# Linear attention gated by a Hadamard feed-forward, all products by Strassen-Winograd: one more feed-forward unit at two levels, and work moved between VectorE and GpSimd

## The chip, the cores and the metric

The kernel runs on one core of a Trainium2 chip. The metric is the device time of one launch in microseconds. The kernel before took 1565.73 us, the median of three runs (1564.98 to 1567.9). In the text, PE is TensorE, DVE is VectorE, ACT is ScalarE, POOL is GpSimd, SP is the engine whose queue issues the transfers. Everything is float32.

## The reference

Eight sequences of 512 tokens with 512 features. Cut to what is computed:

```python
xn = layernorm(x)                                  # (8, 512, 512)
q, k, v = xn @ Wq.T + bq, xn @ Wk.T + bk, xn @ Wv.T + bv
phi_q, phi_k = elu(q) + 1, elu(k) + 1
context = phi_q * cumsum(phi_k * v, axis=tokens) * 32**-0.5
s = context @ Wo.T + bo
h = fwht(xn * SU_ug)                               # Hadamard transform of 512
up, gate = h @ W_up.T * scale_up, h @ W_gate.T * scale_gate       # 2048 wide
d = fwht(silu(gate) * up * SU_dp) @ W_down.T * scale_dp
out = x + s * silu(d)
```

## The kernel before

**Tiling.** The sequences go in four pairs, p = 0 to 3. In a pair one sequence is one half of the tokens of a matrix product and the other sequence the other half, and each product is done with Winograd's form of Strassen's scheme: seven products P1 to P7 instead of eight. `xo` holds the seven combinations of the tokens, a weight tile `w` the seven combinations of a weight; both are made by `encode_tokens` and `encode_weights` (lines 293 to 308, four additions or subtractions each). The Hadamard transforms are folded into the weights, so only the plain scales remain.

**Groups.** `group` (L442) runs one such scheme: 14 matmuls of 128x512, whose results lie in the PSUM banks px (three buffers), py (one) and pz (two), and are put together by ACT copies (`sa_`, `sb_`, `sc_`, L464) and DVE sums (L468). A matmul appears as two records in the profile. `hidden_unit` (L803) with `block_product` (L622) applies the scheme twice: 7 x 7 x 2 = 98 matmuls of 128x256 do what four `group`s (gate and up, two blocks each) do with 56 of 128x512. It reads weights that were encoded at both levels from DRAM: `w_gu` from `d_gu`, seven pieces of 896 KB for each unit.

**A pair.** `attention` runs k, v, q for two groups of heads: a `group`, then `elu_plus_one` on k and q (relu and exp on ACT, L702 and L703, `add, max` on DVE, L704), v times k (POOL, L716), the cumulative sum as a scan on DVE (L722), and its product with q into `co` (DVE L730), which POOL encodes. Then come four units u of the feed-forward, with the output projection after the first; after unit 1 the first half of the down projection, `down(p, 0)`, and after unit 3 the second, `down(p, 1)` (`token_groups`, L528, L539, L543). The first half's sums `dn`, and the projection `s`, go to DRAM (`d_d`, `d_s`) and come back at the end (L750) as `d` and `s`; `y` is the input again. The last steps are silu(d) on ACT, times s on POOL, plus y on DVE, and the store.

**Pair 0 makes the weights.** There a raw weight is loaded (`raw_w`), k, q, v and o weights are encoded on POOL (`first_w`) and kept in DRAM. `folded_w` loads gate and up weights, makes butterflies on DVE (L930 to L933), multiplies with the Hadamard matrix `had` on PE (L939, bank t), copies with the signs on ACT (L945), and encodes. From two such weights `inner_w` makes the second level (DVE L408) in a tile `s_` of the pool `xin` and stores 14 pieces to `d_gu`. So in pair 0 all four units run with `gate` and `up`, that is with `group`s; `up` multiplies gate and up and POOL encodes the result `ho` (L297 to L300). In pairs 1 to 3 all units are `hidden_unit`s. The down weights are folded in the background by `chain_down`, `butterflies_down` (L969), `fold_down` and `down_w`.

**The next pair's tokens.** `normalized(b)` loads a sequence x_b into the pool `xin`, normalizes it and stores it to `d_x`; `next_tokens` reads it back turned (`squares`, L235: four pieces of 256 KB for each sequence, in runs of 128 bytes) as z_b. The even sequence's z lies in `xin`, the odd one's in `t8`; DVE finishes the transposition (L93) into `xo` while the second down half runs.

**What sets the order.** A place is the time of one matmul of 128x512; `at(n, fn)` writes an agenda of steps that are issued n places later, `advance` runs it. `later` puts DVE work on a list that `pace` issues behind DVE's sums, so much for each; `background` gives a lower priority to the scheduler. Weights come in the order of `queue`; `get_w` asks three ahead. Every transfer is issued by SP in order, so one that waits for a buffer holds those behind it. The pools `wpool` (4 tiles), `t8` (6), `xin` (1), `hop` (2) and `snap` (6) set when a buffer comes free.

Of the kernel before, what the change touches and what calls it, by code (L numbers as in the profile page):

```python
# [21 lines left out]
def kernel(  # L22
# [160 lines left out]
    def normalized(b):  # L183

        xt = load_x(b)
        d = dram.tile([L, D], F32, tag=f"d_x_{b}", name=f"d_x_{b}")
        kept[f"x_{b}"] = d

        def store():
            nc.sync.dma_start(d.rearrange("(n p) d -> p n d", p=P), xt)  # L190

        if b > 3:
            layernorm(b, xt)
            store()
            return
        mv = small.tile([P, NT, 2], F32, tag="mv", name=f"mv_{b}")
        rstd = small.tile([P, NT], F32, tag="rstd", name=f"rstd_{b}")

        def stats(t):
            st = small.tile([P, 6], F32, tag="st", name=f"st_{b}_{t}")  # L200
            nc.vector.bn_stats(st, xt[:, t, :])
            nc.vector.bn_aggr(mv[:, t, :], st)

        def root():
            nc.vector.tensor_scalar(rstd, mv[:, :, 1], EPS, None, ALU.add)
            nc.scalar.activation(rstd, rstd, AF.Sqrt)

        def scaled(t):
            if t == 0:
                nc.vector.reciprocal(rstd, rstd)  # L210
            nc.vector.tensor_scalar(
                xt[:, t, :], xt[:, t, :], mv[:, t, 0:1], rstd[:, t : t + 1], ALU.subtract, ALU.mult
            )

        def start():
            for t in range(NT):
                later(0.8, stats, t)
            later(0.3, root)
            for t in range(NT):
                later(0.6, scaled, t)  # L220
            later(0.0, store)

        at(12, start)
# [115 lines left out]
                w = by_factor(w)  # L339
        return w  # L340

    def raw_w(name, src, n0, dn, step, c0, dc):

        w = new_w(name)
        for a in range(2):
            tiles = src[:, c0 + a * dc : c0 + a * dc + P].rearrange("(n p) e -> p n e", p=P)
            for b in range(2):
                n = n0 + b * dn
                place = (P1, P2, P7, P4)[2 * a + b]
                nc.sync.dma_start(w[:, :, place, :], tiles[:, n : n + step + 1 : step])  # L350
        return w
# [41 lines left out]
    def inner_w(m, u, w0, w1):  # L393

        if u not in inner:
            inner[u] = dram.tile([P, 7, 2, 7, P], F32, tag=f"d_gu_{u}", name=f"d_gu_{u}")
        d = inner[u][:, :, ("gate", "up").index(m)]

        def store(c, t):
            nc.sync.dma_start(d[:, :, c, :], t)  # L400

        store(P1, w0[:, 0])
        store(P2, w0[:, 1])
        store(P4, w1[:, 1])
        t = xin.tile([P, 3, 7, P], F32, tag="x", name=f"s_{m}_{u}")

        def made(c, i, a, b, op):
            nc.vector.tensor_tensor(t[:, i], a, b, op)  # L408
            store(c, t[:, i])

        later(1.0, made, P5, 0, w1[:, 0], w1[:, 1], ALU.add, soon=True)
        later(1.0, made, P6, 1, t[:, 0], w0[:, 0], ALU.subtract, soon=True)
        later(1.0, made, P3, 2, w0[:, 1], t[:, 1], ALU.subtract, soon=True)
        later(1.0, made, P7, 0, w0[:, 0], w1[:, 0], ALU.subtract, soon=True)

# [266 lines left out]
    def attention(p, xo, co, get_w):  # L684
        def project(m, g, then):
            w = get_w(m, g)
            r = t8.tile([P, 2, 2, L], F32, tag="t", name=f"{m}_{p}_{g}")
            b = (col("b" + m, g), col("b" + m, g + 2))

            def whole(px):  # L690
                nc.scalar.activation(r[:, 0, 1], px, AF.Identity, bias=b[0])  # L691
                then(r)

            group(
                f"{m}_{p}_{g}", [w[:, 0], w[:, 1]], x_rhs(xo),
                (r[:, 0, 0], r[:, 1, 0], r[:, 1, 1]), whole, b,
            )

        def elu_plus_one(r, name):
            neg = t8.tile([P, 2, 2, L], F32, tag="t", name=f"neg_{name}")  # L700
            for h in range(2):
                nc.scalar.activation(neg[:, h], r[:, h], AF.Relu, scale=-1.0)  # L702
                nc.scalar.activation(neg[:, h], neg[:, h], AF.Exp, scale=-1.0)  # L703
                nc.vector.scalar_tensor_tensor(r[:, h], r[:, h], 1.0, neg[:, h], ALU.add, ALU.max)  # L704

        def heads(g):
            phi = {}

            def with_k(k):
                phi["k"] = k  # L710
                elu_plus_one(k, f"k_{p}_{g}")

            def with_v(v):
                k = phi["k"]
                for h in range(2):
                    nc.gpsimd.tensor_tensor(v[:, h], v[:, h], k[:, h], ALU.mult)  # L716
                at(4, lambda: sums(k, v))

            def sums(k, v):
                for h in range(2):  # L720
                    for s in range(2):
                        nc.vector.tensor_tensor_scan(  # L722
                            k[:, h, s], ones.to_broadcast([P, L]), v[:, h, s], 0.0, ALU.mult, ALU.add
                        )

            def with_q(q):
                k = phi["k"]
                elu_plus_one(q, f"q_{p}_{g}")
                for h in range(2):
                    nc.vector.scalar_tensor_tensor(  # L730
                        co[:, g, h : h + 3 : 2, :], k[:, h], QSCALE, q[:, h], ALU.mult, ALU.mult
                    )
                encode_tokens(nc.gpsimd, co[:, g])

            project("k", g, with_k)
            project("v", g, with_v)
            project("q", g, with_q)

        for g in range(2):
            heads(g)  # L740
# [43 lines left out]
        )  # L784
        return g

    def up(p, f, g, xo, ho, get_w):

        w = get_w("up", f)
        r = t8.tile([P, 2, 2, L], F32, tag="t", name=f"u_{p}_{f}")  # L790

        def with_up(px):
            nc.gpsimd.tensor_tensor(ho[:, P1], g[:, 0, 0], r[:, 0, 0], ALU.mult)  # L793
            nc.vector.tensor_tensor(ho[:, P7], g[:, 0, 1], px, ALU.mult)
            nc.gpsimd.tensor_tensor(ho[:, P2 : P3 + 1 : 2], g[:, 1], r[:, 1], ALU.mult)
            encode_tokens(nc.gpsimd, ho)

        group(
            f"up_{p}_{f}", [w[:, 0], w[:, 1]], x_rhs(xo),
            (r[:, 0, 0], r[:, 1, 0], r[:, 1, 1]), with_up,  # L800
        )
# [114 lines left out]
        eng.tensor_tensor(d[:, :, 0], s[:, :, 0], s[:, :, 1], ALU.add)  # L916
        eng.tensor_tensor(d[:, :, 1], s[:, :, 0], s[:, :, 1], ALU.subtract)

    def folded_w(name, src, f):

        w = raw_w(f"{name}_{f}", src, 0, 2, 1, f * P, NG * P)
        places = (slice(P1, P7 + 1, 2), slice(P2, P4 + 1, 3))
        rs = []

# [101 lines left out]
    def first_w(m, g):  # L1026


        if m == "gate":
            return folded_w(m, wgate_t, g)  # L1030
        if m == "up":
            return folded_w(m, wup_t, g)
        name, eng = f"{m}_{g}", nc.gpsimd
        if m == "o":
            t = new_w(name)
            w = by_factor(t)
            rows_w(w, wo_t, g, 2)
        else:
            t = w = raw_w(name, sources[m], 0, 2, 1, g * P, 2 * P)

        def encode():
            encode_weights(eng, w)
            keep_w(name, t)

        return w, [(5, encode)]

    def later_w(m, g):
        return stream_w((m, g)), []

# [2 lines left out]
    for p in range(B // 2):  # L1052
        queue += [(p, m, g) for g in range(2) for m in ("k", "v", "q")]
        for u in range(NU):
            if p == 0:
                queue += [(p, m, f) for m in ("gate", "up") for f in (u, u + NU)]
            else:
                queue += [(p, "gu", (u, i)) for i in (P1, P5, P6, P2, P7, P3, P4)]
# [7 lines left out]
    def ask(n):  # L1066
        while queue and len(ahead) < n:
            p, m, g = queue.pop(0)
            w, steps = (first_w if p == 0 and m != "down" else later_w)(m, g)
            ahead.append({"key": (m, g), "w": w, "steps": steps, "traced": 0, "asked": 0, "place": 0})  # L1070

    def step_of(e):
# [88 lines left out]
    for p in range(B // 2):  # L1161
# [9 lines left out]
        more = p + 1 < B // 2  # L1171
        hos = []
        for u in range(NU):
            if p == 0:
                gs = [gate(p, u, xo, get_w)]
                gs.append(gate(p, u + NU, xo, get_w))
                if u == 0:
                    project_out(p, co, get_w)
                ho = hop.tile([P, 2, 7, L], F32, tag="h", name=f"ho_{p}_{u}")
                for m in range(2):  # L1180
                    up(p, u + m * NU, gs[m], xo, ho[:, m], get_w)
            else:
                ho = hop.tile([P, 2, 7, L], F32, tag="h", name=f"ho_{p}_{u}")
                hidden_unit(p, u, xo, ho, get_w, u % 2 == 1)
                if u == 0:
                    project_out(p, co, get_w)
            hos.append(ho)
            if more and u < 2:
                with background():
                    normalized(2 * p + 2 + u)  # L1190
            if u == 1:
                down(p, 0, hos, get_w)
                hos = []
        if more:
            catch_up()
# [57 lines left out]
```

## Time and profile before

| | |
|---|---|
| median of three runs | 1565.73 us |
| the profiled execution's own time | 1565.26 us |
| its span | 1563.5 us |
| mean granted TensorE clock | 0.997 |
| share of the span: PE, PEld, DVE, POOL, ACT | 98%, 71%, 61%, 32%, 27% |
| HBM read, written | 189.83 MB, 76.02 MB |

Stretches of the first pair (busy us of each engine):

| stretch, us | what | PE | DVE | ACT | POOL |
|---|---|---|---|---|---|
| 0 to 50 | load, layernorm, first groups | 41.8 | 30.7 | 22.2 | 23.8 |
| 50 to 100 | attention of pair 0 | 46.6 | 48.9 | 23.3 | 23.0 |
| 100 to 150 | end of attention, unit 0 | 42.0 | 42.2 | 21.9 | 19.2 |
| 150 to 264 | units 0 and 1, first down half begins | 114.0 | 81.4 | 35.7 | 38.1 |
| 264 to 355 | down half, unit 2 | 89.7 | 47.3 | 26.6 | 8.1 |
| 355 to 412 | unit 3 | 53.8 | 43.5 | 16.2 | 23.8 |
| 412 to 470 | second down half | 55.8 | 30.0 | 8.6 | 21.1 |
| 470 to 600 | attention of pair 1 and on | 128.1 | 83.3 | 47.6 | 49.6 |

A row of the timeline gives start, length, engine, line, operation, output tile and input tiles, the form, the number of instructions taken together, and in brackets the idle time before them with what ended it. A row of consecutive matmuls is as long as they take, with a modelled end that reaches a little into the next row; what they take in a stream is read from start to start. Idle time counts here only where it lies on TensorE.

### The profile page before, as it was taken

The page shows a single profiled execution, that of the slowest core. Times are in us where ns is not written, and L with a number is a line of the kernel's source. Part 1 is how long each engine was busy: PE and PEld are TensorE (multiplying, and loading weights), DVE is VectorE, ACT ScalarE, POOL GpSimd, SP SyncE. Part 2 cuts the span into 40 slices and gives each one's busy share as a digit, 9 for nine tenths or more (in the row PEclk, how much of TensorE's full clock was granted, in tenths as well). Part 3 has the DMA queues.
Part 4 walks back from the last instruction along what each step waited for, and adds up shares of the span by engine and source line. Part 5 has one row for each costly group of instructions (what it writes and reads, how often), then busy time and mean ns, then how long its engine had stood idle before and what let it go on. Part 6 is the DMA issues. An engine that isn't in the chain of part 4 may idle for free.

```text
span 1563.5 us, 15520 instructions
## 1 busy us (share of the span) xinstructions
PE 1529.6 (98%) x5840; PEld 1105.7 (71%) x5840; DVE 953.9 (61%) x1336; ACT 419.8 (27%) x666; POOL 501.5 (32%) x286
## 2 busy tenths in 40 slices
PE   7989999999999999999999999999999999999998
PEld 4335546744584588888885488888886468888887
DVE  5898784469466674716676574725675476543673
ACT  5453340232114521112215431111212431111211
POOL 4532144014421252304612235301622226110731
PEclk9999999999999999999999999999999999999999
DMA  8244966566885344344575434335474233535462
GB/s 280 83 148 152 285 227 205 185 199 214 229 305 173 89 161 152 110 159 158 157 283 216 101 138 144 139 101 195 151 250 172 82 106 118 185 98 178 152 251 95
DMA packets 196682, 266.86 MB, mean 171 GB/s; under 512 B 56704, under 2 KB 155008, under 8 KB 192384
## 3 DMA queue, kind: packets, MB, share of 16 engines
q1 hardware_dynamic: 196464, 265.84, 51.8%
q8 instruction: 46, 0.75, 0.2%
q14 instruction: 28, 0.23, 0.0%
q10 hardware_dynamic: 144, 0.03, 0.0%
HBM read 189.83 MB, written 76.02 MB: 170 GB/s over the span
## 4 chain that ended last, share of the span: by engine, by line
PE 88%; DVE 4%; DMA 2%; POOL 2%; ACT 2%; issue 2%; SPq 0%; POOLq 0%; DVEq 0%; ACTq 0%
PE px_gu L630 19%; PE px_dn L528 13%; PE pz_gu L630 9%; PE pz_dn L528 6%; PE py_gu L630 5%; PE py_dn L528 4%; PE px_o L528 3%; PE px_up L452 3%; PE px_k L452 3%; PE px_v L452 3%; PE px_gate L452 3%; PE px_q L452 3%; PE pz_o L528 2%; PE pz_q L452 2%; PE pz_k L452 2%
## 5 line engine op out<-in xcount | busy, mean ns | idle before, releaser
L630 PE MATMUL px_gu<-xo,w_gu 128*128 128x256 f32 x1344 | 320.6, 380 | 0.0
L630 PEld LDWEIGHTS px_gu<-xo,w_gu 128*128 128x128 f32 x1344 | 254.7, 190 | 39.9 <-issue 3.6
L528 PE MATMUL px_dn<-w_down,ho 128*128 128x256 f32 x1024 | 228.5, 379 | 0.0
L528 PEld LDWEIGHTS px_dn<-w_down,ho 128*128 128x128 f32 x1024 | 194.5, 190 | 28.2 <-issue 2.1
L630 PE MATMUL pz_gu<-xo,w_gu 128*128 128x256 f32 x672 | 172.9, 380 | 0.0
L831 POOL TENSOR_TENSOR u<-u,v 128x1024 f32<-128x1024 f32 x24 | 56.1, 2359 | 354.2 <-DVE u L668 347.5
L630 PEld LDWEIGHTS pz_gu<-xo,w_gu 128*128 128x128 f32 x672 | 127.2, 190 | 18.4 <-DVE a L672 0.9
L528 PE MATMUL pz_dn<-w_down,ho 128*128 128x256 f32 x496 | 112.7, 380 | 2.7 <-POOL ho L300 2.7
L528 PEld LDWEIGHTS pz_dn<-w_down,ho 128*128 128x128 f32 x496 | 93.6, 190 | 17.9 <-POOL ho L300 3.5
L876 POOL TENSOR_TENSOR s<-s,d 128x512 f32<-128x512 f32 x30 | 40.4, 1346 | 152.8 <-ACT d L875 113.7
L716 POOL TENSOR_TENSOR v<-v,k 128x1024 f32<-128x1024 f32 x16 | 43.0, 2686 | 140.4 <-ACT v L691 112.7
L630 PE MATMUL py_gu<-xo,w_gu 128*128 128x256 f32 x336 | 86.2, 379 | 0.0
L630 PEld LDWEIGHTS py_gu<-xo,w_gu 128*128 128x128 f32 x336 | 63.9, 190 | 8.7
L793 POOL TENSOR_TENSOR ho<-g,u 128x512 f32<-128x512 f32 x8 | 12.5, 1557 | 164.6 <-DVE u L468 154.7
L835 POOL TENSOR_TENSOR v<-v,r 128x1024 f32<-128x1024 f32 x24 | 56.2, 2365 | 25.6 <-DVE r L668 25.6
L452 PE MATMUL px_v<-xo,w_v 128*128 128x512 f32 x128 | 60.8, 594 | 1.5 <-ACT sc_v L464 1.5
L875 ACT ACTIVATE d<-d 128x512 f32<-128x512 f32 x31 | 19.5, 630 | 158.3 <-DVE d L543 116.1
L452 PE MATMUL px_k<-xo,w_k 128*128 128x512 f32 x128 | 60.9, 597 | 1.1 <-ACT sa_k L464 1.0
L452 PE MATMUL px_gate<-xo,w_gate 128*128 128x512 f32 x128 | 59.7, 594 | 0.9 <-ACT sc_gate L462 0.9
L452 PE MATMUL px_q<-xo,w_q 128*128 128x512 f32 x128 | 60.1, 592 | 0.0
L452 PE MATMUL px_up<-xo,w_up 128*128 128x512 f32 x128 | 59.3, 592 | 0.0
L528 PE MATMUL px_o<-w_o,co 128*128 128x256 f32 x256 | 58.4, 379 | 0.0
(263 smaller groups left out, 2464.1 us busy)
## 6 DMA issues: line engine op xcount, KB each, us to landing
w_gu<-d_gu SPq DMA_DIRECT2D x84, 896.0 KB, 4.5
w_down<-d_down SPq DMA_DIRECT2D x56, 512.0 KB, 3.5
d_s<-o SPq DMA_DIRECT2D x8, 1024.0 KB, 4.4
d_d<-dn SPq DMA_DIRECT2D x8, 1024.0 KB, 7.6
d<-d_d SPq DMA_DIRECT2D x8, 1024.0 KB, 6.7
s<-d_s SPq DMA_DIRECT2D x8, 1024.0 KB, 7.9
y<-in_x_dram SPq DMA_DIRECT2D x8, 1024.0 KB, 7.8
out_dram<-y SPq DMA_DIRECT2D x15, 512.0 KB, 3.3
```

What stands on the lines that cost most here:

```text
L452: nc.tensor.matmul(p.rearrange("p a t -> p (a t)") if len(r.shape) == 2 else p, ws[k][:, i, :], r, start=(first and k == 0), stop=(k == n ...
L528: nc.tensor.matmul(p[:, c], t[:, (2 * g + c) * P : (2 * g + c + 1) * P], ws[i](k), start=(first and k == 0 and c == cs[0]), stop=(k == n - ...
L630: nc.tensor.matmul(p[:, lane], w[:, lane, i, :], x[:, i, :], start=(first and lane == 0), stop=True, skip_group_check=True,)
L716: nc.gpsimd.tensor_tensor(v[:, h], v[:, h], k[:, h], ALU.mult)
L793: nc.gpsimd.tensor_tensor(ho[:, P1], g[:, 0, 0], r[:, 0, 0], ALU.mult)
L831: nc.gpsimd.tensor_tensor(r[:, m], ru1[:, m], rv[:, m], ALU.add)
L835: nc.gpsimd.tensor_tensor(rv[:, m], rv[:, m], rr[:, m], ALU.add)
L875: nc.scalar.activation(d, d, AF.Silu)
L876: (nc.vector if final and (a, s) == (1, 0) else nc.gpsimd).tensor_tensor(r, r, d, ALU.mult)
```

## The change

1. **Unit 3 of pair 0** becomes a `hidden_unit`. Its four raw weights are loaded into tiles of `t8` and folded during the first down half of pair 0 by a new function, `weights_ahead(NU - 1)`, which is called ahead of `down(p, 0)`; the queue asks for the seven `gu` pieces instead. The second level of `xo` is made after that down half (`inner_tokens`, three subtractions of 128x1792) and ahead of unit 3 (`inner_t3`, seven).
2. **`normalized(3)`** moves from after unit 1 to the beginning of unit 3, in the background, and takes the plain `layernorm` branch.
3. **k times v** is issued on DVE, each half followed by its two scans, without the four places between; it was on POOL.
4. **The second half of the exponential** of k and q (relu, exp, `add, max`, for q also the product into `co`) comes seven places later.
5. **Encoding** the k, q and v weights in pair 0 moves from POOL to DVE; so does encoding `ho` for the second block of unit 1.
6. `inner_w`'s last piece (P7) comes eight places later.

```diff
-        if b > 3:
+        if b > 2:
             layernorm(b, xt)
             store()
             return
...
-        later(1.0, made, P7, 0, w0[:, 0], w1[:, 0], ALU.subtract, soon=True)
+
+        def last():
+            later(1.0, made, P7, 0, w0[:, 0], w1[:, 0], ALU.subtract, soon=True)
+
+        later(0.0, at, 8, last, soon=True)
...
-        def elu_plus_one(r, name):
+        def elu_plus_one(r, name, then=None):
             neg = t8.tile([P, 2, 2, L], F32, tag="t", name=f"neg_{name}")
-            for h in range(2):
+
+            def half(h):
                 nc.scalar.activation(neg[:, h], r[:, h], AF.Relu, scale=-1.0)
                 nc.scalar.activation(neg[:, h], neg[:, h], AF.Exp, scale=-1.0)
                 nc.vector.scalar_tensor_tensor(r[:, h], r[:, h], 1.0, neg[:, h], ALU.add, ALU.max)
+                if then:
+                    then(h)
+
+            half(0)
+            at(7, lambda: half(1))
...
             def with_v(v):
                 k = phi["k"]
                 for h in range(2):
-                    nc.gpsimd.tensor_tensor(v[:, h], v[:, h], k[:, h], ALU.mult)
-                at(4, lambda: sums(k, v))
-
-            def sums(k, v):
-                for h in range(2):
+                    nc.vector.tensor_tensor(v[:, h], v[:, h], k[:, h], ALU.mult)
                     for s in range(2):
                         nc.vector.tensor_tensor_scan(
...
             def with_q(q):
                 k = phi["k"]
-                elu_plus_one(q, f"q_{p}_{g}")
-                for h in range(2):
+
+                def context(h):
                     nc.vector.scalar_tensor_tensor(
                         co[:, g, h : h + 3 : 2, :], k[:, h], QSCALE, q[:, h], ALU.mult, ALU.mult
                     )
-                encode_tokens(nc.gpsimd, co[:, g])
+                    if h == 1:
+                        encode_tokens(nc.gpsimd, co[:, g])
+
+                elu_plus_one(q, f"q_{p}_{g}", context)
...
-            encode_tokens(nc.gpsimd, ho)
+            encode_tokens(nc.vector if last else nc.gpsimd, ho)
...
-    def folded_w(name, src, f):
-
-        w = raw_w(f"{name}_{f}", src, 0, 2, 1, f * P, NG * P)
+    def folded_w(name, src, f, room=None):
+
+        w = raw_w(f"{name}_{f}", src, 0, 2, 1, f * P, NG * P, room)
...
-        name, eng = f"{m}_{g}", nc.gpsimd
+        name, eng = f"{m}_{g}", nc.gpsimd if m == "o" else nc.vector
...
+    def weights_ahead(u):
+
+        def begin(m, src, f):
+            t = t8.tile([P, 2, 7, P], F32, tag="t", name=f"w_{m}_{f}")
+            _, steps = folded_w(m, src, f, t)
+            place = 10
+            for _, step in steps:
+                at(place, step)
+                place += 7
+
+        at_ = 2
+        for m, src in (("gate", wgate_t), ("up", wup_t)):
+            for f in (u, u + NU):
+                at(at_, lambda m=m, src=src, f=f: begin(m, src, f))
+                at_ += 12
...
-            if p == 0:
+            if p == 0 and u < NU - 1:
                 queue += [(p, m, f) for m in ("gate", "up") for f in (u, u + NU)]
...
-            w, steps = (first_w if p == 0 and m != "down" else later_w)(m, g)
+            w, steps = (first_w if p == 0 and m not in ("down", "gu") else later_w)(m, g)
...
-            if p == 0:
+            if p == 0 and u < NU - 1:
                 gs = [gate(p, u, xo, get_w)]
                 gs.append(gate(p, u + NU, xo, get_w))
...
-                    up(p, u + m * NU, gs[m], xo, ho[:, m], get_w)
+                    up(p, u + m * NU, gs[m], xo, ho[:, m], get_w, u % 2 == 1 and m == 1)
             else:
+                if p == 0:
+                    catch_up()
+                    inner_t3(xo, (P1, P5, P6, P2, P7))
+                    at(9, lambda: inner_t3(xo, (P3, P4)))
+                    with background():
+                        normalized(3)
                 ho = hop.tile([P, 2, 7, L], F32, tag="h", name=f"ho_{p}_{u}")
                 hidden_unit(p, u, xo, ho, get_w, u % 2 == 1)
...
-            if more and u < 2:
+            if more and u < 2 and (p, u) != (0, 1):
                 with background():
                     normalized(2 * p + 2 + u)
             if u == 1:
+                if p == 0:
+                    weights_ahead(NU - 1)
                 down(p, 0, hos, get_w)
+                if p == 0:
+                    inner_tokens(xo)
                 hos = []
```

More of the change, by code (lines that the diff above doesn't have):

```diff
@@ L340, in stream_w, with raw_w @@
         return w
-    def raw_w(name, src, n0, dn, step, c0, dc):
-        w = new_w(name)
+    def raw_w(name, src, n0, dn, step, c0, dc, w=None):
+        w = new_w(name) if w is None else w
         for a in range(2):
@@ L785, in gate, with up @@
         return g
-    def up(p, f, g, xo, ho, get_w):
+    def up(p, f, g, xo, ho, get_w, last):
         w = get_w("up", f)
```

## The prediction

> **What bounds the kernel now.** I read the page first, then TensorE's timeline for its gaps, then the stretches of the start, and last the DMA issues around the end of the first pair. Page:
>
> ```profile
> span 1563.5 us, 15520 instructions
> PE 1529.6 (98%) x5840; PEld 1105.7 (71%) x5840; DVE 953.9 (61%) x1336; ACT 419.8 (27%) x666; POOL 501.5 (32%) x286
> ...
> PE   7989999999999999999999999999999999999998
> ```
>
> TensorE is the bound: 1529.6 of 1563.5 us. Time can go only by fewer matmuls or by closing its gaps. These are all of 0.8 us or more between 20 and 1500 us (start, us, what, [idle before <- releaser]), each row from TensorE's timeline:
>
> ```profile
> 58.19 3.62 PE L452 MATMUL pz_q<-xo,w_q 128*128 128x512 f32 x4 [3.40 <-DVE q L468]
> 61.64 1.88 PE L452 MATMUL pz_k<-xo,w_k 128*128 128x512 f32 x4
> ```
> ```profile
> 107.92 2.46 PE L988 MATMUL pwd<-rd,had 128*128 128x512 f32 x4 [3.16 <-ACT w_gate L945]
> ```
> ```profile
> 144.67 1.99 PE L528 MATMUL pz_o<-w_o,co 128*128 128x256 f32 x8 [2.92 <-DVE g L468]
> ```
> ```profile
> 265.47 1.99 PE L528 MATMUL pz_dn<-w_down,ho 128*128 128x256 f32 x8 [1.33 <-POOL ho L300]
> ```
> ```profile
> 363.54 1.95 PE L939 MATMUL pw_gate<-r_gate,had 128*128 128x512 f32 x4 [3.18 <-DVE r_gate L933]
> 365.33 1.88 PE L452 MATMUL px_gate<-xo,w_gate 128*128 128x512 f32 x4
> ```
> ```profile
> 428.90 2.00 PE L528 MATMUL pz_dn<-w_down,ho 128*128 128x256 f32 x8 [1.35 <-POOL ho L300]
> 431.07 3.29 PE L528 MATMUL py_dn<-w_down,ho 128*128 128x256 f32 x14 [0.18 <-DMA w_down<-d_down]
> ```
> ```profile
> 492.78 1.98 PE L452 MATMUL px_v<-xo,w_v 128*128 128x512 f32 x4 [1.51 <-ACT sc_v L464]
> ```
>
> Three smaller ones (1.04 at 116, 0.89 at 134.6, 1.04 at 470) bring them to 20 us. Behind the gaps of 3.40 and 3.16 the matmuls run at half clock for about 3.4 us (58.19 to 61.64 for 4 records that take 1.72 elsewhere: +1.73; after 107.92: +1.80, by the same reading), while the gap of 3.18 at 363 is followed by 4 records in the usual 1.8. From 493 to 1500 us there is no gap, so pairs 1 to 3 can only lose. The start is VectorE's: 48.9 of 50 us busy.
>
> ```profile
> 50.00:100.00 50.00, 46.60 (x106) 20.22 (x105) 48.89 (x48) 23.29 (x42) 22.98 (x11) 0.97 0.30 95
> ```
>
> **Part 1: unit 3 of pair 0 with the scheme applied twice.** It issues four `group`s of 14 matmuls of 128x512 now, two records each: 112 x 0.43 us (1.72 for 4) = 48.1. A `hidden_unit` issues 98 of 128x256: 196 x 0.216 (1.72 for 8) = 42.3. That is -5.8 on the bound. The four fold pairs (1.72 each) move, with their loads, encodes and stores, into the first down half: same work, moved. In unit 3 the fold gap (3.18) and in the second down half the encode gap (1.35) and 0.18 lose their cause: -4.7. The narrower matmul costs nothing by width in these rows: 8 of 256 take what 4 of 512 take.
>
> New at the unit's start: VectorE issues about 14 us of work between units 2 and 3 (encodes, down-weight factors, 7 x 0.72 of `inner_t3`) against 14.6 us of matmuls queued there, and the unit's 7 loads of 896 KB land in 4.5 each, as in pairs 1 to 3, where no unit has a gap: +1 (0 to 3). The piece P7 that is stored 8 places later goes where its reader is a whole down half away: 0.
>
> **Part 2: the end of pair 0, where I expect a new wait.** `normalized(3)` moves into unit 3. Its x and the z of sequence 2 share the single buffer of `xin`, and SP's order becomes: x_3's store, a w_down, eight z loads, the two d fetches, w_down, s, y. Now z starts before the down half:
>
> ```profile
> 403.94 0.71 SPq L235 DMA_DIRECT2D z<-d_x  x1
> 405.09 2.59 SPq L400 DMA_DIRECT2D d_gu<-s_up  x2
> 407.73 12.83 SPq L235 DMA_DIRECT2D z<-d_x  x7
> 420.60 1.98 SPq L750 DMA_DIRECT2D d<-d_d  x2
> 422.68 1.44 SPq L335 DMA_DIRECT2D w_down<-d_down  x2
> ```
> ```profile
> 427.45 0.69 DVE L539 TENSOR_TENSOR sa_dn<-px_dn,d 128x512 f32<-128x512 f32 x1 [1.87 <-DMA d<-d_d]
> ```
>
> The half's first matmul is at 411.68, 7.7 us after the first z; d lands 15.8 after it and VectorE already waits 1.87 for it. In the changed order the w_down in front of z waits for that first matmul, so z can't start before it (offset 0 to 3, by x_3's store landing). Eight z at 1.83 (12.83 for 7) are 14.6; d lands about 7 after its issue (median 7.2 in 395 to 440): 22 to 25 after the half's first matmul. VectorE's transposes, then the sum that frees bank py, stand behind d's first reader: 4 us more, 26 to 29. TensorE needs that bank about 20 in: by pair 1's own end, which has no gap, the second block's py_dn comes at 804.01 against 780.70, 23.3 in; counting the changed order's matmuls gives 19.8. The stall, 26 to 29 less 20 to 23, is 3 to 9; I take 7, since w_down, issued 2 behind d and 8.35 to land, is late by about the same; bounds 2 and 14 (w_down's own lateness, 5, on top of 9). If a gap this long is followed by half clock as those of 3.40 and 3.16 were, and that of 3.18 wasn't, it costs 1.7 more; that is in the upper bound. The page TensorE: Matmul & The Clock Gate, of the Trainium skill, has the rule (Why this matters for your kernels) that an idle gap of over about 3 us brings the half clock back; by it the sum below would be -9.0 instead of -10.7.
>
> **Part 3: first attention (20 to 150 us).** VectorE gains 4 k*v (1.17 each beside an idle GpSimd by L816's 2.35 for two at 786.03; the GpSimd op means 2.69) and 8 of the 24 weight encodes at about 0.42: +8 in 50 to 100. It loses the contention with GpSimd that slows its two-input ops:
>
> ```profile
> 49.78 4.50 DVE L969 TENSOR_TENSOR rd<-rd 128x1024 f32<-128x1024 f32 x2
> 54.21 3.34 DVE L722 TENSOR_TENSOR_SCAN k<-ones,v 128x512 f32<-128x512 f32 x2
> ```
>
> 4.50 against 2.35 for the same shape in pair 1: about 11 us between 40 and 106 by such rows, of which 3 to 4 belong to co's and o's encodes, which stay. So VectorE nets about 0 and stays full. What changes is order: q's first difference now stands where it is ready near 52, before its bank is wanted at 54 (gap 3.40 and 1.73 gone), and w_gate's copies stand ahead of the silu that held them (3.16 and 1.80 gone), 10.1 in all. New waits, by walking the new order with these durations: ScalarE's sc_v behind k's later half (1.2), q of the second head behind scans and k*v (about 2.5), pz_o behind the s_gate store (about 1). I take 10.1 less 4.7: -5.4. Bounds: -14.9 (the three other gaps here gone too) and +5 (the last two waits 5 each, with clock).
>
> **Part 4: the rest.** 265: encodes on VectorE and two fold pairs in between, -1.3; there VectorE may stand before a raw weight's slot that GpSimd frees: 0 to +3. Start of pair 1: k's later half stands behind sc_v, -1.5 (0 if VectorE's wait for x keeps it). Attentions of pairs 1 to 3: VectorE takes 4.7 us more each but sat idle 3.39 and 2.46 before the scans there waiting for GpSimd, so 0; bounds 0 (no gap to close but the 1.5 counted) and +10 (six heads, each with a gap of 1.7, near the 1.51 at 492.78).
>
> **Sum**: -5.8 -4.7 +1 +7 -5.4 -1.3 -1.5 = -10.7 on the profiled execution, whose time is 1565.26 (span 1563.5 and 1.8 around it), 0.5 under the median 1565.73. That is 1554.6, in the median's frame 1555.
>
> **Rivals.** (a) *All closes*: the stall is at its bound of 2 and the start's gaps go. With the start at -14.9, 1565.7 - 5.8 - 4.7 - 14.9 - 2.8 + 2 = 1539.5; with it at -5.4 and the +1, 1550; half way, 1545. For it: pair 1 ends with the same loads and no gap. Against: it has four of its eight z loaded earlier, and pair 0's d is late already. (b) *The start gives it all back*: part 3 is +1 instead of -5.4: 1561.4. For it: 48.9 of 50. (c) *Slower, by SP's queue at the end of pair 0*: everything there waits in order behind x_3's store, which waits for four background scales on VectorE. Without its stall the sum is -17.7. The 7 stands for a z that starts 1.5 after the half's first matmul, and each us more delays z, d and w_down by one: at 12 the change gains nothing, at 16 it is 1565.7 - 17.7 + 21.5 = 1569.5. For it: scales at background priority have no due time. Against: VectorE was busy 43.5 of 57 us in 355 to 412, with the encodes that leave this stretch. (d) *Attentions of pairs 1 to 3* get the +10: 1565. For it: two VectorE ops more in a chain that evictions wait behind; against: 83.3 of 130 us busy in 470 to 600. (e) That the unit isn't changed at all is excluded: its 98 matmuls stand in the new order.
>
> **How the numbers follow.** Forecast 0.50 (1555, own range 1551 to 1560), (a) 0.15, (b) 0.13, (c) 0.12, (d) 0.10. 0.2% is 3.1 us, about what a measurement here can tell from no change: faster means under 1562.6, slower over 1568.9. Faster: 0.48 + 0.15 + 0.09 + 0.02 = 0.74; slower: 0.10 of (c), 0.03 of (d) and 0.02 of (b): 0.15; same 0.11. The range leaves out half of (a) and most of (c)'s upper part: 1544 to 1568.
>
> **What would show it.** Right: unit 3 as px_gu/pz_gu of 42.3 us, no gap at pw_gate, no q L468 gap near 55, z's first issue at the down half's first matmul, a gap of 5 to 9 at the half's py_dn with d or w_down behind it. Wrong: no such gap (then nearer 1548), or new gaps in 90 to 150 of over 10 in sum, or a gap after 500.

## The result and the profile after

The changed kernel takes 1572.08 us (median of 8 runs, 1569.28 to 1574.43) beside 1567.22 for the kernel before on the same chips: ratio 1.003, 95% interval 1.0018 to 1.0042, that is 3 to 7 us slower. The forecast was 1555 and the range ended at 1568. The two profiled executions lie further apart than the medians, 1571.8 against 1563.5 us of span (granted clock 0.993 against 0.997); the accounting below is of their 8.3 us. Line numbers from here on are those of each kernel's own file: L472 of the changed kernel is L468 of before, L532 is L528, L547 is L543, L634 is L630, L942 is L933.

TensorE's gaps in the changed kernel (TensorE's timeline, rows as before):

```profile
81.81 1.98 PE L456 MATMUL px_v<-xo,w_v 128*128 128x512 f32 x4 [1.76 <-ACT sc_v L468]
104.14 3.39 PE L456 MATMUL px_gate<-xo,w_gate 128*128 128x512 f32 x4 [4.90 <-DVE w_gate L306]
140.78 1.73 PE L948 MATMUL pw_up<-r_up,had 128*128 128x512 f32 x2 [2.31 <-DVE r_up L942]
216.58 1.95 PE L948 MATMUL pw_up<-r_up,had 128*128 128x512 f32 x4 [1.31 <-DVE r_up L942]
261.14 2.86 PE L532 MATMUL pz_dn<-w_down,ho 128*128 128x256 f32 x12 [0.93 <-DVE u L472]
309.73 1.96 PE L948 MATMUL pw_gate<-r_gate,had 128*128 128x512 f32 x4 [2.17 <-DVE r_gate L942]
375.55 1.13 PE L634 MATMUL pz_gu<-xo,w_gu 128*128 128x256 f32 x4 [3.98 <-DVE u L472]
```

and the end of pair 0 with the start of pair 1:

```profile
438.77 1.22 PE L532 MATMUL py_dn<-w_down,ho 128*128 128x256 f32 x2 [6.03 <-DVE d L547]
439.78 6.18 PE L532 MATMUL px_dn<-w_down,ho 128*128 128x256 f32 x16
```
```profile
478.49 3.23 PE L456 MATMUL px_k<-xo,w_k 128*128 128x512 f32 x4 [1.90 <-ACT sa_k L468]
```

The old gaps at 58, 108, 145, 364, 429 and 493 are gone, and those at 265 and 470 are now 0.93 and 1.90. Seven new ones of 1.3 to 6 us stand elsewhere, and several are followed by half clock: the 16 records after 439.78 take 6.02 us to the next row (445.80) instead of 3.45. Nearly all of it is over by 500 us: pair 1's first `hidden_unit` starts at 545.53 against 537.52, 8.0 late, and the span ends 8.3 late.

The chain at the end of pair 0, VectorE's read of d:

```profile
434.46 0.69 DVE L543 TENSOR_TENSOR sa_dn<-px_dn,d 128x512 f32<-128x512 f32 x1 [8.94 <-DMA d<-d_d]
```

and SP's queue (issues and the time they took to issue):

```profile
410.55 0.37 SPq L190 DMA_DIRECT2D d_x<-x  x1
412.33 0.32 SPq L335 DMA_DIRECT2D w_down<-d_down  x1
415.05 6.33 SPq L235 DMA_DIRECT2D z<-d_x  x5
```

x_3's store is issued at 410.55, the first z at 415.05, 2.9 us after the half's first matmul (412.14), and d is there 22.3 after it. Before, the first z was 7.7 ahead of that matmul.

### The profile page after: what moved, and what is told of

Same layout as the page of the kernel before. It is cut to its first block, busy times and chain, and to the rows that moved or that the text cites. A ratio compares the mean times of both kernels' runs of the same rounds, so it can differ in the third digit from the quotient of the medians.

```text
span 1571.8 us, 15701 instructions
## 1 busy us (share of the span) xinstructions
PE 1530.6 (97%) x5924; PEld 1126.4 (72%) x5924; DVE 1003.0 (64%) x1423; ACT 419.2 (27%) x664; POOL 424.0 (27%) x236
## 4 chain that ended last, share of the span: by engine, by line
PE 82%; DVE 10%; DMA 3%; issue 2%; ACT 1%; SPq 1%; POOL 1%; POOLq 0%; DVEq 0%; ACTq 0%
PE px_gu L634 19%; PE px_dn L532 11%; PE pz_gu L634 9%; PE pz_dn L532 5%; PE py_gu L634 5%; PE px_o L532 4%; PE px_k L456 3%; PE py_dn L532 3%; PE px_v L456 3%; PE px_q L456 3%; PE px_gate L456 2%; PE pz_o L532 2%; PE px_up L456 2%; PE pz_k L456 1%; PE pz_q L456 1%
## 5 line engine op out<-in xcount | busy, mean ns | idle before, releaser
L634 PE MATMUL px_gu<-xo,w_gu 128*128 128x256 f32 x1456 | 348.4, 381 | 0.1
L634 PEld LDWEIGHTS px_gu<-xo,w_gu 128*128 128x128 f32 x1456 | 276.9, 191 | 44.5 <-issue 5.0
L532 PE MATMUL px_dn<-w_down,ho 128*128 128x256 f32 x1024 | 231.2, 382 | 0.0
L532 PEld LDWEIGHTS px_dn<-w_down,ho 128*128 128x128 f32 x1024 | 196.4, 192 | 29.5 <-issue 2.4
L634 PE MATMUL pz_gu<-xo,w_gu 128*128 128x256 f32 x728 | 187.6, 380 | 5.3 <-DVE u L472 4.0
L634 PEld LDWEIGHTS pz_gu<-xo,w_gu 128*128 128x128 f32 x728 | 138.1, 190 | 26.4 <-DVE u L472 4.4
L532 PE MATMUL pz_dn<-w_down,ho 128*128 128x256 f32 x496 | 112.4, 379 | 0.9 <-DVE u L472 0.9
L532 PEld LDWEIGHTS pz_dn<-w_down,ho 128*128 128x128 f32 x496 | 93.7, 190 | 15.4 <-DVE u L472 1.3
L634 PE MATMUL py_gu<-xo,w_gu 128*128 128x256 f32 x364 | 93.4, 379 | 0.0
L297 POOL TENSOR_TENSOR co<-co 128x512 f32<-128x512 f32 x8 | 10.2, 1272 | 265.8 <-DVE co L736 265.8
L634 PEld LDWEIGHTS py_gu<-xo,w_gu 128*128 128x128 f32 x364 | 69.2, 190 | 9.4
L532 PE MATMUL py_dn<-w_down,ho 128*128 128x256 f32 x256 | 58.7, 382 | 6.0 <-DVE d L547 6.0
L830 ACT ACTIVATE a<-a,cols_sb 128x512 f32<-128x512 f32 x26 | 18.8, 722 | 156.5 <-DVE a L672 154.7
L532 PE MATMUL px_o<-w_o,co 128*128 128x256 f32 x256 | 58.4, 379 | 0.0
L532 PEld LDWEIGHTS py_dn<-w_down,ho 128*128 128x128 f32 x256 | 48.8, 191 | 13.0 <-DVE d L547 6.4
```

Source lines behind the costliest of these rows:

```text
L297: eng.tensor_tensor(o[..., P5, :], o[..., P7, :], o[..., P1, :], ALU.subtract)
L532: nc.tensor.matmul(p[:, c], t[:, (2 * g + c) * P : (2 * g + c + 1) * P], ws[i](k), start=(first and k == 0 and c == cs[0]), stop=(k == n - ...
L634: nc.tensor.matmul(p[:, lane], w[:, lane, i, :], x[:, i, :], start=(first and lane == 0), stop=True, skip_group_check=True,)
L830: nc.scalar.activation(g[:, m], g[:, m], AF.Silu, scale=col("w_gate", u + m * NU + a * NG))
```

## The experiments

Ratios are to runs of the kernel before on the same chip, with 95% intervals.

**The two halves of the change alone.** `attention_alone` is the kernel before with these lines of the change (cut):

```diff
-            for h in range(2):
+            half(0)
+            at(7, lambda: half(1))
...
-                    nc.gpsimd.tensor_tensor(v[:, h], v[:, h], k[:, h], ALU.mult)
+                    nc.vector.tensor_tensor(v[:, h], v[:, h], k[:, h], ALU.mult)
...
-        name, eng = f"{m}_{g}", nc.gpsimd
+        name, eng = f"{m}_{g}", nc.gpsimd if m == "o" else nc.vector
```

`unit3_alone` is the changed kernel without them.

> The kernel before with the attention parts alone: k*v on VectorE, the second half of the exponential seven places later, the weight encodes of k, q and v on VectorE; unit 3 of pair 0, x_3 and inner_w as before. Theory (read from the gaps of the two profiles): this half of the change gains 2 us by 184 us (landmark 186.34 to 184.09), loses about 1 at the start of pair 1, where sa_k came late after the stall in front of it and not by these parts, so here 0, and nothing in pairs 1 to 3: 2 to 3 us faster than before. Rival (the rest of the loss, the fold waits of 1.3 to 2.2 us behind VectorE at 216 and 309, also comes from VectorE's added work): 0 to 2 us slower. As predicted before the result: 5.4 and 1.5 faster, 6.9.

> The changed kernel with the attention parts undone (k*v and the weight encodes back on GpSimd, both halves of the exponential at once); unit 3 with the scheme twice, x_3 in unit 3, the folds in the first down half stay. Theory: the loss is all here. 1.1 + 3.98 + 0.36 + 0.5 with 1.5 of half clock at the start of unit 3, 6.03 with 3.15 of half clock in the second down half, 3.4 in the folds of the first, against 5.8 + 3.2 + 1.4 + 0.2 gained: 6 to 10 us slower than before, gaps at pz_gu and py_dn as in the changed kernel. Rival (the attention parts fill VectorE and so make the gaps): those gaps shrink, and it is faster than before by up to 10.

`attention_alone`: 0.9968 (0.9956 to 0.998), about 5 us faster, more than expected. The gaps of 3.40, 3.16 and 1.51 are gone; it has new ones of 1.74 at 82 and 4.81 at 104, and 2.31 at 141 is what is left of the 2.92 at 145. `unit3_alone`: 1.005 (1.0036 to 1.0063), about 8 us slower. It has the gaps at pz_gu and py_dn, the latter even longer, from TensorE's timeline:

```profile
377.97 1.16 PE L634 MATMUL pz_gu<-xo,w_gu 128*128 128x256 f32 x4 [3.98 <-DVE u L472]
```
```profile
443.17 1.22 PE L532 MATMUL py_dn<-w_down,ho 128*128 128x256 f32 x2 [8.00 <-DVE d L547]
```

So the loss lies in the half that has less work for TensorE, and the attention's moves were not its cause.

**The chain from x_3's store.** `x3_urgent` takes one thing from the changed kernel:

```diff
-                    with background():
-                        normalized(3)
+                    normalized(3)
```

> The changed kernel with one line less: normalized(3) in unit 3 without the background priority, so that VectorE's four scales and x_3's store come earlier and the z loads of the second down half start ahead of w_down. Theory (the wait is a chain from x_3's store through SP's queue to z, d and bank py): z starts 10 us or more earlier, VectorE's wait of 8.94 for d and TensorE's gap of 6.03 go to under 2, and the half clock behind it (3.15) too: 7 to 10 us faster than the changed kernel, 2 to 5 faster than before. Rival 1 (the transfers themselves are the limit: eight z in runs of 128 bytes, d, s, y, w_down in one stretch): z starts earlier and the gap stays over 4, now behind w_down; 0 to 3 faster. Rival 2: VectorE waits for x_3's load ahead of the sums of unit 3, a new gap of 2 or more there.

0.9943 (0.9931 to 0.9955): 1559.84 us beside 1568.09, about 9 us faster than before, and by the two ratios 13 to 14 faster than the changed kernel, more than the 7 to 10 expected. SP's queue:

```profile
392.27 0.37 SPq L190 DMA_DIRECT2D d_x<-x  x1
394.05 0.32 SPq L327 DMA_DIRECT2D w_gu<-d_gu  x1
397.39 0.66 SPq L235 DMA_DIRECT2D z<-d_x  x1
```

and VectorE's read of d, which waits for TensorE only:

```profile
426.25 0.69 DVE L543 TENSOR_TENSOR sa_dn<-px_dn,d 128x512 f32<-128x512 f32 x1 [1.22 <-PE px_dn L532]
```

x_3 is stored 18 us earlier and z starts 18 us earlier. The gap of 6.03 and its half clock are gone, and so is the one at the start of pair 1: from 377 us to the tail this kernel has no gap of 0.3 us or more. That is also the excess over the 7 to 10: the gap at the start of pair 1 (1.90, with half clock behind it) and those of 0.50 and 0.32 in unit 3 went with the stall. The transfers are the same ones; it was their start, not their number. Neither rival showed.

**The start of unit 3.** TensorE waits 3.98 there for the sum `u<-sb_up,pz_up`. VectorE's rows in front of it, in the changed kernel:

```profile
359.48 1.48 DVE L293 TENSOR_TENSOR xo<-xo 128x256 f32<-128x256 f32 x1
360.89 0.67 DVE L472 TENSOR_TENSOR u<-sb_up,pz_up 128x512 f32<-128x512 f32 x1
361.49 2.91 DVE L93 TENSOR_TENSOR wd<-wd 128x256 f32<-128x256 f32 x2
364.32 2.89 DVE L293 TENSOR_TENSOR xo<-xo 128x256 f32<-128x256 f32 x2
...
372.08 2.48 DVE L333 TENSOR_TENSOR wd<-wd 128x256 f32<-128x256 f32 x4
374.49 0.41 DVE L293 TENSOR_TENSOR xo<-xo 128x256 f32<-128x256 f32 x1
374.82 0.67 DVE L472 TENSOR_TENSOR u<-sb_up,pz_up 128x512 f32<-128x512 f32 x1
```

The same operation of 128x256 takes 0.41 and 1.48 us; the long ones lie beside GpSimd's products and encodes of unit 2's `ho`, as in its rows:

```profile
359.37 1.32 POOL L297 TENSOR_TENSOR ho<-ho 128x512 f32<-128x512 f32 x1 [1.02 <-DVE ho L803]
361.71 2.40 POOL L804 TENSOR_TENSOR ho<-g,u 128x1024 f32<-128x1024 f32 x1 [1.02 <-DVE u L472]
364.19 1.33 POOL L298 TENSOR_TENSOR ho<-ho 128x512 f32<-128x512 f32 x1
```

Two explanations: contention, or what stands in the queue. `ho2_dve` takes the encodes from GpSimd:

```diff
-                    up(p, u + m * NU, gs[m], xo, ho[:, m], get_w, u % 2 == 1 and m == 1)
+                    up(p, u + m * NU, gs[m], xo, ho[:, m], get_w, (u, m) == (1, 1) or u == 2)
```

> The changed kernel with the encoding of unit 2's ho (eight operations of 128x512) on VectorE instead of GpSimd. It takes GpSimd's operations away from beside VectorE between 364 and 381 us, and gives VectorE 8 x 0.69 = 5.5 us more work there. Theory (the gap of 3.98 at pz_gu comes from contention: the 128x256 operations took 1.45 instead of 0.42 us, 7.7 us too long in all between 357 and 375): those operations fall to 0.42 wherever GpSimd is quiet, the added work eats the gain, gap 2 to 5, time within 2 us of the changed kernel. Rival (VectorE simply has too much work there, the long operations are chance): durations stay, gap 7 to 9, time 4 to 8 us longer.

1.0022 (1.001 to 1.0034), 1571.36 us: like the changed kernel. VectorE's timeline there:

```profile
365.17 0.41 DVE L293 TENSOR_TENSOR xo<-xo 128x256 f32<-128x256 f32 x1
365.51 0.68 DVE L298 TENSOR_TENSOR ho<-ho 128x512 f32<-128x512 f32 x1
```

The `xo` operations fall to 0.41 where GpSimd is quiet, while the two `wd` operations beside the one GpSimd product that is left (2.40 from 362.56) still take 2.91. So their length was contention, and the eight encodes fill the time won. The gap is 3.04 instead of 3.98, in the expected bounds. The page SBUF — State Buffer of the Trainium skill, Who interferes with whom, says that a VectorE operation with two SBUF inputs contends with a GpSimd operation that reads SBUF; 1.48 against 0.41 us agrees.

`x_wd15` leaves GpSimd alone and takes from x3_urgent's queue the encodes of the second half's down weights:

```diff
-    for n, u, j in ((16, 2, 0), (17, 2, 1), (18, 3, 0), (19, 3, 1)):
+    for n, u, j in ((15, 2, 0), (16, 2, 1), (17, 3, 0), (18, 3, 1)):
```

> x3_urgent with the encoding of the second half's down weights one group earlier (places 15 to 18 of the plan, 16 to 19 otherwise). In x3_urgent six of its operations of 128x256 (two at L99, four at L333) stand in VectorE's queue right in front of the sum u<-sb_up,pz_up for which TensorE waits 3.98 at 376; here none does. Theory now (what stands in the queue ahead of that sum sets the gap, contention is the smaller part): the gap falls to 1.5 or less, its half clock (1.5) goes, 3 to 5 us faster than x3_urgent. Rival (contention with GpSimd, or the sheer work, sets it): gap 3 to 4, time within 1.5 us of x3_urgent. A price that could eat it: the earlier loads and their encodes meet the folds, 0 to 2.

0.9982 (0.9973 to 0.9992): 6 us slower than x3_urgent, a miss. The one gap became four of 1.40, 0.40, 0.77 and 0.74, and a new one came, from TensorE's timeline and SP's:

```profile
385.88 2.08 PE L634 MATMUL px_gu<-xo,w_gu 128*128 128x256 f32 x4 [5.33 <-DMA w_gu<-d_gu]
```
```profile
375.61 0.39 SPq L129 DMA_DIRECT2D x<-in_x_dram  x1
376.11 3.93 SPq L327 DMA_DIRECT2D w_gu<-d_gu  x3
```

In the new order x_3's load, which waits for the last piece of `s_up` to leave the single buffer of `xin`, stands ahead of three w_gu loads. `x_wdbg` keeps x3_urgent's order on SP there, with one w_gu load ahead of x_3's, and gives the sixteen encodes a lower priority:

```diff
-                later(0.5, nc.vector.tensor_tensor, w[:, o], w[:, a], w[:, b], op)
+                later(0.5, quiet, w[:, o], w[:, a], w[:, b], op)
...
+        def quiet(*args):
+            with background(150):
+                nc.vector.tensor_tensor(*args)
```

> x3_urgent with the sixteen encodes of the second half's down weights at background priority: the last four leave the place in front of u<-sb_up,pz_up and come in the middle of unit 3, SP's order around w_gu stays, so the mistake of x_wd15 (w_gu behind x's load) isn't repeated. Theory (VectorE's queue ahead of that sum is about 8 operations of 128x256 too long, 0.4 to 0.6 us each): 2.5 us less in front of it, the gap of 3.98 falls to 1 to 2 and its half clock goes: 2 to 4 us faster than x3_urgent. Rival (the last d_down store, now behind z, makes w_down_0 late): a new gap of 2 or more near 415, no gain.

0.9951 (0.9938 to 0.9964): no faster than x3_urgent. What was foreseen of the gap came true, and was given back behind it, from TensorE's timeline:

```profile
372.57 1.13 PE L638 MATMUL pz_gu<-xo,w_gu 128*128 128x256 f32 x4 [1.70 <-DVE u L476]
383.09 1.13 PE L638 MATMUL pz_gu<-xo,w_gu 128*128 128x256 f32 x4 [1.61 <-DVE v L669]
```

with 0.58 at 386 and twice 0.78 at 411 and 413, all behind VectorE. VectorE is busy 51.3 of 60 us in 360 to 420 here, against 39.8 before the change: which sum is late is a matter of order, and that one is late is a matter of load. So both explanations hold in part: the order moves the gap (3.98 to 1.70), contention adds to the load, and no run here takes the cost away. How much of it is contention was not separated further.

**Which of the attention's moves counts.** Each was undone in x3_urgent, then two and all three.

> x3_urgent with k*v back on GpSimd, four places ahead of the scans. Theory: k*v on VectorE is a part of the gap of 4.5 at 104 (scans and k*v stand ahead of the encode of w_gate there, about 6 us with GpSimd beside them) and closes the gap at 55 (3.40 and its half clock) and that of 1.51 at the start of pair 1: undoing it costs 1 to 4 us. Rival (VectorE is full there, so k*v on GpSimd is better at 104 and the gap at 55 was closed by the encodes' move): 1 to 4 us faster.

> x3_urgent with both halves of the exponential issued at once. Theory: the gap of 1.75 at 82 (sc_v behind the later half on ScalarE) goes, and the one of 1.51 behind sc_v at the start of pair 1 comes back: within 2 us of x3_urgent. Rival (the later half is what lets q's first difference be early and closes the gaps at 55 and 108): 4 to 8 us slower.

> x3_urgent with the encodes of k, q and v weights in pair 0 on GpSimd again. Theory: GpSimd's 24 operations slow VectorE's two-input operations between 40 and 60 as they did before (4.50 against 2.35 for two): the gap at 55 comes back in part, 2 to 4 us slower. Rival (fewer operations on VectorE shorten the gap of 4.5 at 104): 1 to 3 us faster.

> x3_urgent with all three attention parts undone. attention_alone was 3.7 us faster than before and unit3_alone 4 us slower than the changed kernel, yet undoing any one of the three in x3_urgent cost 1 us at most. Theory (each of the moves alone takes enough of GpSimd from beside VectorE, so they stand in for one another): 3 to 5 us slower than x3_urgent, with gaps of 3 to 4 at 55 and 108 as before. Rival (the three were needed only because of the stall at the end of pair 0): within 1 us of x3_urgent.

> x3_urgent with both k*v and the encodes on GpSimd, only the later half of the exponential kept. Theory (either of the two on VectorE closes the gap at 55; both on GpSimd bring the contention back): gap of 3 to 4 at 55, 2 to 5 us slower than x3_urgent, like x_none. Rival (the later half alone closes it): within 1 us of x3_urgent.

| undone in x3_urgent (0.9943; 1.75 at 82, 4.49 at 104) | ratio to before | interval | gaps between 50 and 120 us |
|---|---|---|---|
| k*v (`x_kv_pool`) | 0.9949 | 0.9933 to 0.9966 | 0.66 at 56, 2.43 at 67, 4.26 at 108 |
| exponential (`x_exp_once`) | 0.9946 | 0.9931 to 0.9961 | 1.18 at 81, 4.82 at 103 |
| weight encodes (`x_enc_pool`) | 0.9940 | 0.9923 to 0.9956 | 2.64 at 67, 1.89 at 104 |
| k*v and encodes (`x_kv_enc_pool`) | 0.9957 | 0.9945 to 0.9969 | 3.40 at 58, 3.15 at 108, 0.87 at 114 |
| all three (`x_none`) | 0.9974 | 0.9964 to 0.9984 | 3.26 at 60, 1.44 at 70, 3.17 at 110, 1.26 at 118 |

No single one can be told from none. With both k*v and the encodes on GpSimd the gap for q's difference is back, as expected, though the time is only 2 us longer and the intervals overlap. All three undone cost about 5 us, clear of noise. So they stand in for one another. The traces show how only in part: VectorE starts q's difference at 57.4 with both on GpSimd, at 55.4 with k*v alone there, at 53.7 with the encodes alone and at 53.1 in x3_urgent. With the encodes on GpSimd the two `rd` additions ahead of it take 2.35 as in x3_urgent; with k*v there they take 4.50 as before the change, but VectorE no longer waits 3.60 for GpSimd's v. What contention and what waiting and order count was not separated.

The expectations for x_kv_pool (1 to 4 us) and x_enc_pool (2 to 4 slower) missed that. The one for x_exp_once was right in time, but the 1.51 at the start of pair 1, which was to come back, did not, nor did it in x_none.

x_enc_pool's 1.89 at 104, for 4.49, is not all a gain. x_wdbg_enc, with the same edit in this stretch, has 3.59 there (from TensorE's timeline, first x_enc_pool, then x_wdbg_enc):

```profile
67.31 3.63 PE L456 MATMUL px_k<-xo,w_k 128*128 128x512 f32 x4 [2.64 <-ACT sc_k L468]
103.75 2.54 PE L456 MATMUL px_gate<-xo,w_gate 128*128 128x512 f32 x4 [1.89 <-DVE w_gate L306]
```
```profile
66.37 1.96 PE L460 MATMUL px_k<-xo,w_k 128*128 128x512 f32 x4 [2.51 <-ACT sc_k L472]
102.82 3.22 PE L460 MATMUL px_gate<-xo,w_gate 128*128 128x512 f32 x4 [3.59 <-DVE w_gate L306]
```

Half clock follows the first gap in the one and not in the other, TensorE reaches the second gap 1.7 later, and that gap is 1.70 shorter: VectorE, whose encode ends it, is 36.6 us behind the first row in both. So half clock ahead of a gap that another engine sets cost nothing here. The encodes on GpSimd are worth 0.9 at 104 (4.49 to 3.59); they bring the gap at 67, and the 1.75 at 82 is gone.

**P7, eight places later.** `x_p7_once` is x3_urgent with that piece at once:

```diff
-        def last():
-            later(1.0, made, P7, 0, w0[:, 0], w1[:, 0], ALU.subtract, soon=True)
-
-        later(0.0, at, 8, last, soon=True)
+        later(1.0, made, P7, 0, w0[:, 0], w1[:, 0], ALU.subtract, soon=True)
```

`x_p7_enc` also puts the weight encodes back on GpSimd, and `x_p7_wdbg_enc` does that and takes x_wdbg's lower priority; `x_wdbg_enc` is x_wdbg with the weight encodes on GpSimd.

> x3_urgent with inner_w's last piece (P7) made at once, as before the change, instead of eight places later. The prediction costed that move at nothing. Theory: the later piece's store stands in SP's queue ahead of the loads of w_up (201.40 in the changed kernel, 190.47 before), VectorE's butterflies wait 5.25 for them and TensorE 1.3 at 217, in every run that has the move and in none without: undone, the gap at 217 goes; in unit 3 the order of the stores moves too. 1 to 3 us faster than x3_urgent. Rival (the gap at 217 comes from the queue of weights, not from this piece): gap stays, same time within 1 us.

> x_wdbg with the encodes of k, q and v weights on GpSimd again (x_enc_pool had gaps of 2.64 and 1.89 in place of 1.75 and 4.49). If both gains are independent: 1 to 2 us faster than x_wdbg, 1556 or less beside a before of 1568.

> x_p7_once with the encodes of k, q and v weights on GpSimd again. If the gains of the two add: 1 to 2 us faster than x_p7_once, about 1556 beside a before of 1568.

> x_wdbg_enc with P7 at once. If it adds as in x_p7_once: 1 to 3 us faster than x_wdbg_enc (0.9936 of before), about 0.992. If the order of the down weights' stores moves with it and w_down comes late, no gain.

`x_p7_once`: the gap at 217 is gone, and that of 2.1 at 310 too. In the changed kernel P7's store stands in SP's queue ahead of both w_up's loads, and VectorE's butterflies wait for them (SP's timeline, then VectorE's):

```profile
201.40 0.52 SPq L400 DMA_DIRECT2D d_gu<-s_up  x1
202.01 10.05 SPq L350 DMA_DIRECT2D w_up<-in_wup_t_dram  x8
```
```profile
213.34 0.69 DVE L939 TENSOR_TENSOR r_up<-w_up 128x512 f32<-128x512 f32 x1 [5.25 <-DMA w_up<-in_wup_t_dram]
```

Yet nothing is won by it. In the first down half another gap came in place of 0.83, with 1.7 of half clock behind it: VectorE waits for the load of a weight that is folded ahead there, and TensorE's sum stands behind the butterflies (VectorE's timeline, then TensorE's):

```profile
256.89 0.69 DVE L935 TENSOR_TENSOR r_gate<-w_gate 128x512 f32<-128x512 f32 x1 [5.83 <-DMA w_gate<-in_wgate_t_dram]
```
```profile
263.17 4.48 PE L528 MATMUL pz_dn<-w_down,ho 128*128 128x256 f32 x12 [3.32 <-DVE u L468]
```

From px_gate at 104 to px_gate at 312 both kernels take the same time (104.31 to 311.91 in x3_urgent, 105.44 to 313.19 here). In unit 3 x_p7_once loses: its ratio is 0.9972 (0.9962 to 0.9983), 4 to 5 us slower than x3_urgent. x_3's statistics, urgent now, stand in front of TensorE's sum and wait for x_3's load (VectorE's timeline, then TensorE's):

```profile
377.34 1.29 DVE L140 BATCH_NORM_STATS2 st<-x 128x6 f32<-128x512 f32 x2 [5.49 <-DMA x<-in_x_dram]
```
```profile
379.33 1.22 PE L630 MATMUL pz_gu<-xo,w_gu 128*128 128x256 f32 x2 [6.55 <-DVE u L468]
```

That is the second rival of x3_urgent, one edit later. `x_p7_enc` is at 0.9971 and `x_p7_wdbg_enc` at 0.9970, with the same two gaps (3.51 and 6.45, 3.52 and 6.59); the gains that were expected of the three did not come. `x_wdbg_enc` is at 0.9936 (0.9924 to 0.9948), 1558.16 us, and `x_enc_pool` at 0.9940, 1558.37: about 10 us faster than before and 14 faster than the changed kernel, not to be told apart.

## Why the prediction was wrong, step by step

Against the two profiled executions, in us:

| step of the prediction | predicted | measured | from |
|---|---|---|---|
| unit 3's matmuls | -5.8 | -5.8 | 196 records for 112, counted; x_wdbg at the same clock of 0.997 has TensorE busy 1523.7 for 1529.6 |
| fold, encode and w_down gaps closed | -4.7 | -4.7 | 3.18, 1.35, 0.18 gone |
| start of unit 3 | +1 (0 to 3) | +6.7 | 0.36, 3.98 and 1.5 of half clock; later in the unit 0.50 and 0.32 |
| z, d and py at the end of pair 0 | +7 (2 to 14) | +9.2 | 6.03 and 3.15 of half clock |
| first attention | -5.4 | -2.4 | 14.9 of gaps and clock gone, 12.5 new |
| first down half and P7 | -1.3, 0 | +3.1 | 1.31 (at 217) and 2.17 new, 0.93 instead of 1.33 |
| start of pair 1 | -1.5 | +1.1 | 1.90 and 1.7 of half clock for 1.04 and 1.51 |
| pairs 1 to 3 | 0 | 0 | no gap over 0.2 after 500 |
| sum | -10.7 | +7.2 | span +8.3; 1.1 is not placed |

The sum is missed by 19.0 on the spans: 5.7 at the start of unit 3, 4.4 around the first down half, 3.0 in the first attention, 2.6 at the start of pair 1, 2.2 at the end of pair 0, and 1.1 not placed.

- **The end of pair 0 was right**, in place, cause, order and size: z 2.9 after the half's first matmul (0 to 3 foreseen), d 22.3 after it (22 to 25), a gap of 6.03 (5 to 9). Half clock added 3.15 where 1.7 stood in the bounds. `x3_urgent` shows the cause. Its stall was measured at 6.03, 6.78 and 8.00 in three kernels that have it.
- **The largest failed step is "+1 (0 to 3)" at the start of unit 3.** It set 14 us of VectorE work against 14.6 us of matmuls and took durations from rows where GpSimd is quiet. Beside GpSimd the operations of 128x256 took up to 1.49, about 7 us more between 357 and 375, where VectorE was busy 17.97 of 18 us, and the sum TensorE needs at 375 stood behind nine of them that came after its matmuls were done at 369.7. Balanced work hides nothing when the last operation in the queue is the one waited for. `ho2_dve` shows the contention and `x_wdbg` the order; the share of each stays open.
- **"Same work, moved" for the folds failed**, and the -1.3 beside it; the 0 for P7 hangs together with them. P7 was priced by its reader alone and not by what its store stands in front of on SP. Late, it brings 1.31 at 217, where VectorE waits 5.25 for w_up's load behind that store, and 2.17 at 310. At once (`x_p7_once`), VectorE waits 5.83 for the load of a weight that is folded ahead, and TensorE loses 3.32 there and 1.7 of half clock. Up to 312 the two orders take the same time. So the 0 for the piece itself came out, by luck, and a stretch that was to gain 1.3 loses about 3 in either order; `attention_alone`, with P7 at once and no folds moved, has only the old 1.34 there.
- **The first attention was mis-sized.** The gaps named did go (3.40, 3.16), and the contention with them: the two `rd` additions that took 4.50 take 2.35 (at 46.90). Of the new waits only the first came as named, 1.76 behind sc_v (1.2 foreseen). The scans and k*v stood in front of w_gate's encode and not of q's sum, which made 4.90 where 2.5 was put, with half clock of 1.5; and in place of pz_o's wait (1) came 2.31 at pw_up, behind a fold's butterfly, with half clock too. The contention that VectorE was to lose is only needed to go in part: the moves stand in for one another.
- **The start of pair 1**: 1.51 went, as foreseen, but the later half of the exponential is not shown to be the reason, since it is also gone in x_exp_once and x_none, where that half isn't later. Why it went stays open. sa_k's gap grew behind the stall and is gone in x3_urgent, which makes it a sequel.
- Rival (c), slower by SP's queue, named the right place; with 9.2 its stall alone stayed below the 17.7 of gains that it would have had to eat. The steps above supplied the rest.

## What to carry to other kernels

A step given a low priority delays not only itself but every transfer that is queued behind its store on an in-order queue: look for its first reader, and then for what stands behind it. When work moves to an engine that is near full, price each operation beside its neighbour engine, and ask which operation comes last, not whether the sums balance. After each repair read the order again: here all three kernels that joined P7 at once to the urgent x_3 were about 4 us slower than the urgent x_3 alone.

## What was not expected of the hardware

Half clock does not need a gap of 3 us. In the changed kernel it follows gaps of 1.90 (478.49: 4 records take 3.03 to the next row instead of 1.72) and of 2.31 (8 records after 142.30 take 2.86 instead of 1.73), while before the gaps of 2.92 and 3.18 were followed by full speed, as was 2.17 at 309.73 here. After the gap of 6.03 it cost 3.15, which is 6.3 us of half clock instead of 3.4. The page TensorE: Matmul & The Clock Gate of the Trainium skill (Why this matters for your kernels) sets about 3 us of idle time as the limit; these rows differ on both sides, and the measurement decides. So each gap of about 2 to 5 us was a risk of some 1.5 to 1.8 us here, not a sure cost. It differs between executions of one kernel too: of 64 runs of the kernel before beside these experiments, 36 had a granted clock of 0.996 or more and took 1567.0 us on average, 28 had 0.995 or less and took 1569.7.
